# Node ranges of six edge tiles, groups of twelve, and one bank layout for both factors of K

## The chip, the cores and the metric

The kernel runs on one core of one Trainium2 chip. The metric is the device time of one execution in microseconds (us); several executions are timed, and the median counts.

## The reference

One layer of graph attention with 12500 nodes and 212500 edges, 128 features, 8 heads of 16 features, followed by a batch norm, a residual and a layer norm. The edges are sorted by their destination `dst`. Cut to what matters:

```python
Q, K, V = x @ WQ, x @ WK, x @ WV              # per node, split into 8 heads
Eh = edge_attr @ WE                           # per edge
score = K[src] * Q[dst] / 4 * Eh              # per edge and feature
score = exp(clip(score.sum(-1), -5, 5))       # per edge and head
wV = segment_sum(V[src] * score, dst)         # per node
Z = segment_sum(score, dst)
h = x + wV / (Z + 1e-6)
y = batch_norm(h) over the nodes              # mean and variance over all 12500 nodes
return layer_norm(x + y)
```

## The kernel before

**Tiles, ranges, groups.** The edges lie in T = 1661 tiles of 128, an edge on each partition. A range of nodes (`WN` = 64 nodes at most) takes `U` = 4 consecutive tiles, and a group is two ranges, `G` = 8 tiles; a range's nodes are found by one-hot matrices, so the ranges follow the sorted edges. There are 208 groups, the last of them with 5 tiles. A second path for edges that don't fit the ranges hangs on a flag and doesn't run here.

**Table stage.** TensorE multiplies the node columns `hx` by `w_kv` (line 900), ScalarE and VectorE copy the results out (`evac`, lines 454 and 455), and SyncE stores them to the table `kvd` in HBM, a row of K and V (1 KB) for each node, 512 nodes in each of 25 steps. Meanwhile POOL fetches rows of `x` for the first `NX` = 8 groups. These are turned by TensorE (`turn_x`, line 470) and projected (`project`, line 477) into K and V directly: three early groups in pieces of four tiles inside the table stage, at the steps that the list `piece` sets, the other five (called late here) inside the main loop, one group ahead of use. The list `steps` puts small setup jobs between the table's steps (`locate`, `place`, `locate_ring`, the first loads and `turned_onehot`).

**Fetches.** For each later group `load_kv` queues one indirect DMA for each tile (`gather`, line 290) on POOL: 128 rows of `kvd` by the indices `srcs`. The rows land in a slot of SBUF for eight tiles; there are `NSLOT` = 8 slots, and one more (`first`), which serves the table stage until group 6 is through. Four slots first hold `x` for two groups each. A slot goes back to the list `free` when `message(g)` has read it, or, for `x`, when the second of its two groups is projected (line 480). From group 12 on `pace` ties each queued fetch to a step of the iteration in which it is queued; what is queued is taken in order by POOL. In some groups the last tile isn't fetched: ScalarE copies node columns (`fetch_cols`, line 383, 32 a group) that TensorE then projects (`cols_mm`, line 420), VectorE does the same at 12 columns a group (`fetch_v`, line 364), and SyncE fetches rows one by one (`fetch_rows`, 8 a group).

**Main loop.** In iteration g VectorE makes `products(g)` (line 790: K times the edge factor out of two banks `ps_e`, then times the query factor out of two banks `ps_q`), `scores(g)` (797), the clip (806), `turned_onehot(g + 2)` (738), the share of group g - 2 (842 to 849), `onehot(g + 1)` (730 and 731), `message(g)` (812) and `fetch_v`. TensorE makes the factors of group g + 1 (`eh_mm`, 765, and `qe_mm`, 774), `cols_mm`, the sum `add_x(g - 3)` (858), the queries (748) and `gather_sum(g - 1)` (833). ScalarE makes the exponentials (807 into the bank `ps_m`, 808) and the copies of sums. The edge attributes `ea` come by SyncE, 1 MB for two groups (line 700); the places `rb` of the nodes, which `turned_onehot` compares, come from HBM too (line 600).

**PSUM.** Eight banks: three of `ps_e`, two of `ps_q`, `ps_m` (exponentials), `ps_i` (the index row `iota` for the one-hot) and `ps_a` (sums and queries).

**Order.** The order on each engine is that of the program; each engine takes its own instructions in that order, and semaphores join them.

**The end.** After the last group VectorE aggregates the statistics, and the last stage forms residual and layer norm for 25 blocks of 512 nodes. The summed nodes that had been stored to `hT` come back into free slots (`load_x`).

## Time and profile before

| | us |
|---|---|
| runs shown, median of 3 | 2052.56 (2050.99 to 2053.51) |
| the profiled execution | 2056.0 |
| its span | 2054.1 |
| TensorE matmul busy | 1612.4 (78%) |
| VectorE busy | 1645.6 (80%) |
| ScalarE busy | 1046.3 (51%) |
| POOL busy | 1535.1 (75%) |

PE is TensorE's matmul, PEld its weight load, DVE VectorE, ACT ScalarE, POOL GpSimd, SP SyncE. Busy is the sum of an engine's instructions; a bound can stand in a queue that is not busy all the time, since the step from one instruction to the next counts too. In a row of the timeline the bracket is the idle time ahead of it and what ended it; "issue" means that the profile shows nothing that the engine waited for. An fp32 matmul stands as two instructions.

### The profile page before, as it was taken

Reading aid. Unit: us, or ns where it says so; the run is one execution under the profiler, and the core shown is the slowest. Engines: PE = TensorE matmul, PEld = TensorE weight load, DVE = VectorE, ACT = ScalarE, POOL = GpSimd, SP = SyncE. Lnnn points to the kernel's source line nnn. Section 1 sums busy time; section 2 is a strip of 40 time slices with the busy share of each in tenths; the row PEclk is TensorE's granted clock in tenths of the full one; section 3 lists DMA queues with packets and bytes.
Section 4 is the critical chain, followed back from the end, with each engine's and each line's share of the span. In section 5 each row is a group of like instructions: output and inputs, shape, how many; then the busy total and the mean of one; then the engine's idle time right before and its main releaser. Section 6 shows DMA issues by size and latency. Waiting matters only on the chain.

```text
span 2054.1 us, 58951 instructions
## 1 busy us (share of the span) xinstructions
PE 1612.4 (78%) x12867; PEld 1300.0 (63%) x12867; DVE 1645.6 (80%) x5263; ACT 1046.3 (51%) x8290; POOL 1535.1 (75%) x1618
## 2 busy tenths in 40 slices
PE   7889888878777787777787877887877777777777
PEld 6777666666555665665566665666666666655666
DVE  4468999998887788788787887877877787877787
ACT  2245656664554555455455455454555555555436
POOL 7677777777777777777777777777777777777775
PEclk9899989998898888888888889888888898888899
DMA  7856655665555555555555556555555555555573
GB/s 262 294 174 186 205 184 174 200 203 168 172 184 176 173 184 168 175 183 168 181 182 178 170 170 190 179 162 186 184 159 187 183 158 185 165 178 184 170 245 128
DMA packets 130284, 377.69 MB, mean 184 GB/s; under 512 B 36112, under 2 KB 47547, under 8 KB 116091
## 3 DMA queue, kind: packets, MB, share of 16 engines
q0 software_dynamic: 74912, 203.26, 33.2%
q1 hardware_dynamic: 51816, 169.43, 24.2%
q14 instruction: 267, 2.18, 0.3%
q8 instruction: 103, 1.69, 0.3%
q10 hardware_dynamic: 3186, 1.13, 0.2%
HBM read 348.25 MB, written 25.44 MB: 182 GB/s over the span
## 4 chain that ended last, share of the span: by engine, by line
DVE 27%; DMA 25%; PE 20%; issue 19%; POOL 5%; ACT 2%; DVEq 2%; ACTq 0%; SPq 0%; POOLq 0%
DMA slot<-kvd,srcs 23%; DVE slot L790 9%; DVE s L797 8%; PE ps_q L774 5%; POOL slot L290 5%; PE ps_e L765 4%; PE ps_a L833 3%; DVE xv L364 2%; DVE ot L738 2%; PE ps_a L858 1%; DVEq L364 1%; DVE msg L812 1%; PE ps_e L900 1%; DVE s L806 1%; PE ps_q L900 1%
## 5 line engine op out<-in xcount | busy, mean ns | idle before, releaser
L290 POOL DMA_INDIRECT slot<-kvd,srcs x1518 | 1445.7, 952 | 467.0 <-issue 282.3
L383 ACT ACTIVATE xc<-hx 128x1 f32 x6272 | 647.0, 190 | 176.8 <-issue 142.6
L765 PE MATMUL ps_e<-w_e,ea 128*128 128x128 f32 x3322 | 496.7, 301 | 215.7 <-DVE slot L790 206.2
L765 PEld LDWEIGHTS ps_e<-w_e,ea 128*128 128x128 f32 x3322 | 431.6, 205 | 281.5 <-DVE slot L790 238.2
L774 PE MATMUL ps_q<-qs,ot 64*128 64x128 f32 x3322 | 374.3, 338 | 166.8 <-DVE slot L790 153.8
L790 DVE TENSOR_TENSOR slot<-slot,ps_e 128x512 f32<-128x512 f32 x410 | 273.2, 679 | 239.2 <-DMA slot<-kvd,srcs 202.0
L774 PEld LDWEIGHTS ps_q<-qs,ot 64*128 64x128 f32 x3322 | 303.5, 230 | 228.2 <-DVE slot L790 211.4
L833 PE MATMUL ps_a<-msg,oh 128*64 128x136 f32 x3322 | 316.5, 316 | 1.9 <-DVE msg L812 1.7
L807 ACT ACTIVATE ps_m<-s 128x64 f32<-128x64 f32 (+1 forms) x209 | 47.6, 228 | 500.6 <-DVE s L806 471.2
L797 DVE TENSOR_REDUCE s<-slot 128x64 f32<-128x1024 f32 (+1 forms) x208 | 249.9, 1202 | 19.4 <-DVE slot L790 0.9
L790 DVE TENSOR_TENSOR slot<-slot,ps_q 128x512 f32<-128x512 f32 x410 | 261.5, 678 | 1.0 <-PE ps_q L774 0.7
L833 PEld LDWEIGHTS ps_a<-msg,oh 128*64 128x64 f32 x3322 | 202.9, 150 | 88.4 <-issue 68.4
L812 DVE TENSOR_TENSOR msg<-slot,ps_m 128x1024 f32<-128x1024 f32 (+2 forms) x209 | 247.8, 1187 | 2.1 <-ACT ps_m L807 1.3
L876 ACT ACTIVATE ring<-ps_a 128x64 f32 x408 | 90.7, 222 | 155.1 <-PE ps_a L833 139.1
L364 DVE COPY xv<-hx 128x1 f32 x2304 | 155.8, 143 | 0.0
L731 DVE TENSOR_TENSOR oh<-ps_i,rel 128x512 f32<-128x512 f32 x208 | 141.7, 681 | 0.0
L858 PE MATMUL ps_a<-ident,at 128*128 128x128 f32 x408 | 112.5, 365 | 0.9 <-ACT os L838 0.9
L719 ACT ACTIVATE xw<-hx 128x64 f32 x416 | 82.4, 245 | 41.7 <-issue 23.6
L858 PEld LDWEIGHTS ps_a<-ident,at 128*128 128x128 f32 x408 | 81.6, 231 | 28.9 <-issue 5.6
L748 PE MATMUL ps_a<-w_q,xw 128*128 128x128 f32 x416 | 96.8, 321 | 0.4 <-ACT qs L752 0.4
L859 PE MATMUL ps_a<-xw,ident 128*128 128x128 f32 x408 | 95.8, 324 | 0.0
L738 DVE TENSOR_SCALAR ot<-rbq,wiota 128x512 f32<-128x512 uint8 x188 | 95.3, 507 | 0.0
(187 smaller groups left out, 1471.7 us busy)
## 6 DMA issues: line engine op xcount, KB each, us to landing
ea<-eaT SPq DMA_DIRECT2D x103, 1024.0 KB
byrow<-kvd SPq DMA_DIRECT2D x1536, 1.0 KB
slot<-kvd,srcs POOLq DMA_INDIRECT x1518
rbq<-relT SPq DMA_DIRECT2D x94, 128.0 KB
kvd<-slot SPq DMA_DIRECT2D x12, 512.0 KB
kvd<-t SPq DMA_DIRECT2D x12, 512.0 KB
ring<-xT SPq DMA_DIRECT2D x24, 256.0 KB
hT<-ring SPq DMA_DIRECT2D x23, 256.0 KB
```

What stands on the lines that cost most here:

```text
L290: return nc.gpsimd.indirect_dma_start(out=out, out_offset=None, in_=table, in_offset=bass.IndirectOffsetOnAxis(ap=part(SRC, e, 1), axis=0))
L364: nc.vector.tensor_copy(XV[k][:, r % P:r % P + 1], hx[:, ds(off, 1)])
L383: nc.scalar.activation(XC[k][:, r % P:r % P + 1], hx[:, ds(off, 1)], AF.Copy)
L731: by(("one", g), nc.vector.tensor_tensor(one, iota_ps[:, None, :WN].to_broadcast([P, k, WN]), r[:, :, None].to_broadcast([P, k, WN]), op=O ...
L738: by(("ot", g), nc.vector.tensor_scalar(OT[g], RB[g], wiota, None, op0=OP.is_equal))
L765: by(("eh", g), nc.tensor.matmul(t[:, j - a, :], EA[g][:, j, :], w_e, start=True, stop=True))
L774: by(("qe", g), nc.tensor.matmul(QE[g][h][:, j, :], OT[g][r, j * P:(j + 1) * P], QS[g][r], start=True, stop=True))
L790: step = nc.vector.tensor_tensor(kv, kv, of[g][i][:, :b - a, :], op=OP.mult)
L797: step = nc.vector.tensor_reduce(SS[g][:, a:b, :], KV[g](a, b, 0).rearrange("p t (h d) -> p t h d", d=DH), axis=AX.X, op=OP.add)
L812: step = nc.vector.tensor_tensor(MSG[g][:, a:b, :P].rearrange("p t (h d) -> p t h d", d=DH), KV[g](a, b, P).rearrange("p t (h d) -> p t h ...
L833: by(("sum", g), nc.tensor.matmul(AGG[g][h * WN:(h + 1) * WN], OH[g][h * n + j], MSG[g][:, h * n + j, :], start=(j == 0), stop=(j == k - 1)))
L858: nc.tensor.matmul(ps, AT[g], ident, start=True, stop=False)
```

## The change

`U` becomes 6 and `G` 12, so that a range of 64 nodes takes six tiles and there are 139 groups instead of 208. The constants that count groups are rescaled: `NX` 6, so 72 tiles come from `x` (64 before), `NSLOT` 5 slots of twelve tiles (12 KB in each partition, 8 KB before), `LATE` 6. The fetch rates per tile are kept: 48 columns a group for ScalarE in three loads of 16, 18 for VectorE, 12 rows for SyncE. `EARLY` stays at 3 groups, which are now nine pieces of four tiles. The edge attributes are loaded for each group, 768 KB.

The two factors of K share six banks of four tiles (`FULL_BANKS`): four of `ps_e`, two of `ps_q`; two of the banks hold two tiles of each factor. `products` runs over the banks, one instruction for each where the tiles lie in a slot (for a late group, whose K and V lie in pieces of four tiles, two for some banks). The bank `ps_i` is gone: `iota` lies in `ps_m`, and so do the results of `cols_mm`, which were in a bank `ps_e`.

Core of the diff:

```diff
-G = 8
-U = 4
+G = 12
+U = 6
+B = 4
 WN = 64
 CH = 512
-NSLOT = 8
-NX = 8
+NSLOT = 5
+NX = 6
 EARLY = 3
-RUN = 64
+RUN = 48
 ROWS = P
-LATE = 8
+LATE = 6
 RQ = 4
 SEC = RUN * U
 RING = 1024
 MARGIN = 64
 PAD = 2 * MARGIN + WN
-COLS = 32
+COLS = 48
 LOAD = 16
-FIRST_COL = 8
+FIRST_COL = 6
 COL_LAG = 3
-SP_ROWS = 8
-FIRST_ROW = 8
+SP_ROWS = 12
+FIRST_ROW = 6
 ROW_LAG = 2
...
+FULL_BANKS = [("ps_e", (0, 1, 2, 3), "eeee"), ("ps_e", (4, 5, 6, 7), "qqee"), ("ps_e", (8, 9, 10, 11), "eeqq"),
+              ("ps_e", (4, 5, 10, 11), "eeee"), ("ps_q", (0, 1, 2, 3), "qqqq"), ("ps_q", (6, 7, 8, 9), "qqqq")]
...
-    small_ps = psp.tile([P, 4, P], F32, name="ps_m", bufs=1)
+    small_ps = psp.tile([P, 4 * P], F32, name="ps_m", bufs=1)
     sum_ps = psp.tile([P, 4 * P], F32, name="ps_a", bufs=1)
-    iota_ps, spare_ps = psp.tile([P, 4, P], F32, name="ps_i", bufs=1)[:, 0, :], sum_ps[:, W + P:W + 2 * P]
+    iota_ps, spare_ps = small_ps[:, 2 * P:3 * P], sum_ps[:, W + P:W + 2 * P]
 
     def exp_ps(g):
-        c = (g % 2) * G * H
-        return small_ps[:, 3, c:c + G * H].rearrange("p (t h) -> p t h", h=H)
+        c = 4 * P - (g % 2 + 1) * G * H
+        return small_ps[:, c:c + G * H].rearrange("p (t h) -> p t h", h=H)
 
 
...
-    first = slot(NSLOT).rearrange("p (h c d) -> p h c d", h=2, d=2 * P)
+    first = slot(NSLOT).rearrange("p (h c d) -> p h c d", c=B, d=2 * P)
 
     def table_tile(q):
-        return first[:, q % 4] if q % 4 < 2 else tab.tile([P, 4, 2 * P], F32, name="t", bufs=2)
+        return first[:, q % 6] if q % 6 < 3 else tab.tile([P, B, 2 * P], F32, name="t", bufs=3)
...
-            PAIRS[g] = edge_bank(g).rearrange("p a b -> p (a b)")[:, :2 * P]
+            PAIRS[g] = small_ps[:, :2 * P]
...
-        return psp.tile([P, 4, P], F32, name="ps_e", bufs=3)
+        return psp.tile([P, 4, P], F32, name="ps_e", bufs=PSUM["ps_e"])
...
-        if a and (g % 2 or g == nxg - 1):
+        if a == G - B and (g % 2 or g == nxg - 1):
...
-        for t in range(ustarts[r[0]], end, P):
-            n = min(P, end - t)
+        for t in range(ustarts[r[0]], end, P // G * G):
...
-                turned_of = wp.tile([P, P], F32, name="relby", bufs=1)
+                turned_of = xt_tile()[:, 0, :]
...
+    def banks(g):
+        if nt(g) == G:
+            return FULL_BANKS
+        return [(name, range(a, b), kind * (b - a)) for name, kind in (("ps_e", "e"), ("ps_q", "q"))
+                for a, b in halves(g)]
+
     def load(i):
...
-        gs = range(2 * i, min(2 * i + 2, NG))
-        if not gs:
-            return
-        t, n = wp.tile([P, 2, G, P], F32, name="ea", bufs=2), sum(nt(g) for g in gs)
-        assert nt(2 * i) == G or len(gs) == 1
-        for k, g in enumerate(gs):
-            EA[g] = t[:, k]
-        nc.sync.dma_start(t.rearrange("p c a b -> p (c a b)")[:, :n * P],
-                          eaT[:, starts[2 * i] * P:(starts[2 * i] + n) * P])
+        EA[i] = wp.tile([P, G, P], F32, name="ea", bufs=2)
+        nc.sync.dma_start(EA[i].rearrange("p a b -> p (a b)")[:, :nt(i) * P],
+                          eaT[:, starts[i] * P:(starts[i] + nt(i)) * P])
...
-        half = [table_tile(2 * (g % 2) + a) for a in (0, 1)]
-        KV[g] = lambda a, b, c, n=P: half[a // 4][:, a % 4:a % 4 + b - a, c:c + n]
-        for a in (0, 4):
+        part = [table_tile(3 * (g % 2) + a) for a in range(G // B)]
+        KV[g] = lambda a, b, c, n=P: part[a // B][:, a % B:a % B + b - a, c:c + n]
+        for a in range(0, G, B):
...
+    BANK, FACTOR = {}, {}
...
-        EH[g] = []
-        for a, b in halves(g):
-            t = edge_bank(g)
-            for j in range(a, b):
-                by(("eh", g), nc.tensor.matmul(t[:, j - a, :], EA[g][:, j, :], w_e, start=True, stop=True))
-            EH[g].append(t)
+        BANK[g] = []
+        for name, tiles, kinds in banks(g):
+            BANK[g].append(psp.tile([P, B, P], F32, name=name, bufs=PSUM[name]))
+            for k, (j, kind) in enumerate(zip(tiles, kinds)):
+                FACTOR[kind, g, j] = BANK[g][-1][:, k, :]
+                if kind == "e":
+                    by(("eh", g), nc.tensor.matmul(FACTOR["e", g, j], EA[g][:, j, :], w_e, start=True, stop=True))
     def qe_mm(g):
-        QE[g] = [psp.tile([P, 4, P], F32, name="ps_q", bufs=2) for _ in (0, 1)]
         for j in range(U):
             for h in (0, 1):
                 if j < usizes[2 * g + h]:
                     r = slice(h * WN, (h + 1) * WN)
-                    by(("qe", g), nc.tensor.matmul(QE[g][h][:, j, :], OT[g][r, j * P:(j + 1) * P], QS[g][r],
-                                                   start=True, stop=True))
+                    by(("qe", g), nc.tensor.matmul(FACTOR["q", g, h * usizes[2 * g] + j],
+                                                   OT[g][r, j * P:(j + 1) * P], QS[g][r], start=True, stop=True))
...
-        return halves(g) if g < nxg and g not in SLOT else [(0, sizes[g])]
-
-    def products(g, hs=(0, 1)):
-        for of in (EH, QE):
-            for i in hs:
-                a, b = halves(g)[i]
-                kv = KV[g](a, b, 0)
-                step = nc.vector.tensor_tensor(kv, kv, of[g][i][:, :b - a, :], op=OP.mult)
-                PARTS.setdefault(g, []).append(step)
+        return [(a, a + B) for a in range(0, G, B)] if g < nxg and g not in SLOT else [(0, sizes[g])]
+
+    def in_runs(g, tiles):
+        runs = [[tiles[0], tiles[0] + 1]]
+        for j in tiles[1:]:
+            if j == runs[-1][1] and (g in SLOT or j % B):
+                runs[-1][1] += 1
+            else:
+                runs.append([j, j + 1])
+        return runs
+
+    def products(g, which=None):
+        for i, (_, tiles, _) in enumerate(banks(g)):
+            if which is not None and i not in which:
+                continue
+            by_k, runs = BANK[g][i][:, :len(tiles), :], in_runs(g, tiles)
+            if g in SLOT and len(runs) == 2:
+                (a, b), (c, d) = runs
+                n = b - a
+                assert c - a == G // 2 and d - c == n
+                kv = KV[g](0, G, 0).rearrange("p (h t) d -> p h t d", h=2)[:, :, a:b, :]
+                step = nc.vector.tensor_tensor(kv, kv, by_k.rearrange("p (h t) d -> p h t d", h=2), op=OP.mult)
+            else:
+                k = 0
+                for a, b in runs:
+                    kv = KV[g](a, b, 0)
+                    step = nc.vector.tensor_tensor(kv, kv, by_k[:, k:k + b - a, :], op=OP.mult)
+                    k += b - a
+            PARTS.setdefault(g, []).append(step)
...
-    for k in range(2 * early):
-        piece.setdefault(3 + k * (NQ - 4) // (2 * early), []).append((k // 2, 4 * (k % 2)))
+    for k in range(G // B * early):
+        piece.setdefault(3 + k * (NQ - 4) // (G // B * early), []).append((k // (G // B), B * (k % (G // B))))
...
-        if g % 2:
-            load((g - 1) // 2 + 2)
+        within(load, g + 2)
...
-            turn_x(g + 1, 0, True)
-            turn_x(g + 1, 4, True)
+            for a in range(0, G, B):
+                turn_x(g + 1, a, True)
...
-            for step in (SENT[g - 1], PARTS[g][1], BY["eh", g + 1], PARTS[g][3], PARTS[g][4], BY["qe", g + 1]):
+            for step in (SENT[g - 1], PARTS[g][0], PARTS[g][1], BY["eh", g + 1], *PARTS[g][2:7], BY["qe", g + 1]):
...
-        fetch_cols(g, 1)
+        for k in range(1, COLS // LOAD):
+            if k > 1:
+                load_cols(g, k)
+            fetch_cols(g, k)
...
-    products(g, (0,))
+    products(g, (0, 1, 2))
```

Three places in the order of the built programs, where the argument rests.

POOL at the end of the fetches from `x` (table `x`, indices `srcs`), with what each instruction waits for (DMAHW and DMASW are transfers, DVE is VectorE). Before:

```order
L290 DMA slot_124<-x,srcs 128x128 [waits DMASW5_49,DVE_49]
L290 DMA slot_124<-x,srcs 128x128 [waits DMASW6_49]
L290 DMA slot_124<-x,srcs 128x128 [waits DMASW7_49,DVE_49]
L290 DMA slot_631<-kvd,srcs 128x256 [waits DMAHW4_49,DMAHW3_49,DMAHW5_49,DMAHW2_49,DMAHW6_49,DMAHW1_49,DMAHW7_49,DMAHW0_49,DMASW0_49]
L290 DMA slot_631<-kvd,srcs 128x256 [waits DMASW1_49]
```

And after:

```order
L295 DMA slot_122<-x,srcs 128x128 [waits DMASW6_49]
L295 DMA slot_122<-x,srcs 128x128 [waits DMASW7_49]
L295 DMA slot_786<-kvd,srcs 128x256 [waits DMAHW3_49,DMAHW4_49,DMAHW2_49,DMAHW5_49,DMAHW1_49,DMAHW6_49,DMAHW0_49,DMAHW7_49,DMASW0_49,DVE_49]
L295 DMA slot_786<-kvd,srcs 128x256 [waits DMASW1_49]
L295 DMA slot_786<-kvd,srcs 128x256 [waits DMASW2_49]
```

The first fetch from `kvd` waited for transfers alone; it now carries a wait on VectorE too, the last reader of its slot. Two groups' fetches (16) stood ready before without such a wait on `message`; the slots of the first two groups are now freed by `message(0)` and `message(1)`.

VectorE behind the table's end, group 0 (`oh` is the one-hot, `ot` its counterpart by node, `s` the scores). Before:

```order
L730 TENSOR_TENSOR oh<-rel,lim 128x1
L731 TENSOR_TENSOR oh<-ps_i,rel 128x512
L790 TENSOR_TENSOR slot_195<-slot_195,ps_e 128x4x128 [waits PE_49] x2
L790 TENSOR_TENSOR slot_195<-slot_195,ps_q 128x4x128 [waits DVE_49,PE_49] x2
L797 TENSOR_REDUCE s<-slot_195 128x64 [waits DVE_49]
L806 TENSOR_SCALAR s<-s 128x64 [waits DVE_49]
L738 TENSOR_SCALAR ot<-rb,wiota 128x512 [waits DMAHW6_49,DMAHW5_49]
L730 TENSOR_TENSOR oh<-rel,lim 128x1
L731 TENSOR_TENSOR oh<-ps_i,rel 128x512
L812 TENSOR_TENSOR msg<-slot_195,ps_m 128x8x128 [waits Activation_49]
```

And after:

```order
L735 TENSOR_TENSOR oh<-rel,lim 128x1
L736 TENSOR_TENSOR oh<-ps_m,rel 128x768
L811 TENSOR_TENSOR slot_192<-slot_192,ps_e 128x4x128 [waits PE_49] x3
L806 TENSOR_TENSOR slot_192<-slot_192,ps_e 128x2x2x128 [waits DVE_49]
L811 TENSOR_TENSOR slot_192<-slot_192,ps_q 128x4x128 x2
L819 TENSOR_REDUCE s<-slot_192 128x96 [waits DVE_49]
L828 TENSOR_SCALAR s<-s 128x96 [waits DVE_49]
L743 TENSOR_SCALAR ot<-rb,wiota 128x768 [waits DMAHW7_49,DMAHW0_49]
L735 TENSOR_TENSOR oh<-rel,lim 128x1
L736 TENSOR_TENSOR oh<-ps_m,rel 128x768 [waits Activation_49]
L834 TENSOR_TENSOR msg<-slot_192,ps_m 128x12x128
```

The same steps in the same order, with six products instead of four, over 12 tiles instead of 8; the one-hot reads `iota` in `ps_m` and waits for ScalarE, whose exponentials go to that bank.

VectorE in an iteration with `cols_mm` (16 before, 12 after), from the clip on (`rz`, `at` are the share of group g - 2). Before:

```order
L806 TENSOR_SCALAR s<-s 128x64 [waits DVE_49]
L738 TENSOR_SCALAR ot<-rbq,wiota 128x512
L842 TENSOR_SCALAR rz<-os 128x8 [waits Activation_49]
L845 RECIPROCAL rz<-rz 128x8 [waits DVE_49]
L849 SCALAR_TENSOR_TENSOR at<-os,keep,rz 128x128 [waits DVE_49,PE_49]
L730 TENSOR_TENSOR oh<-rel,lim 128x1 [waits PE_49]
L731 TENSOR_TENSOR oh<-ps_i,rel 128x512
L812 TENSOR_TENSOR msg<-slot_1399,ps_m 128x8x128 [waits Activation_49]
```

And after:

```order
L828 TENSOR_SCALAR s<-s 128x96 [waits DVE_49]
L743 TENSOR_SCALAR ot<-rbq,wiota 128x768
L864 TENSOR_SCALAR rz<-os 128x8 [waits Activation_49]
L867 RECIPROCAL rz<-rz 128x8 [waits DVE_49]
L871 SCALAR_TENSOR_TENSOR at<-os,keep,rz 128x128 [waits DVE_49,PE_49]
L735 TENSOR_TENSOR oh<-rel,lim 128x1 [waits PE_49]
L736 TENSOR_TENSOR oh<-ps_m,rel 128x768 [waits PE_49]
L834 TENSOR_TENSOR msg<-slot_1715,ps_m 128x12x128
```

The one-hot had no wait of its own; it now waits for TensorE, which writes the result of `cols_mm` into the same bank.

## Rows read from the trace of the kernel before

**Rows 1.** Page: busy us (share) xcount; a group: busy us, mean ns | idle.

```profile
PE 1612.4 (78%) x12867; PEld 1300.0 (63%) x12867; DVE 1645.6 (80%) x5263; ACT 1046.3 (51%) x8290; POOL 1535.1 (75%) x1618
...
L290 POOL DMA_INDIRECT slot<-kvd,srcs x1518 | 1445.7, 952 | 467.0 <-issue 282.3
```

**Rows 2.** Timeline, POOL, head and end: start us, duration us, what, [idle before].

```profile
3.21 1.15 POOL L290 DMA_INDIRECT slot<-x,srcs  x1 [2.04 <-DMA srcs<-src]
...
85.32 0.94 POOL L290 DMA_INDIRECT slot<-x,srcs  x1 [0.30 <-issue]
...
90.95 0.94 POOL L290 DMA_INDIRECT slot<-kvd,srcs  x1 [4.69 <-issue]
92.20 0.95 POOL L290 DMA_INDIRECT slot<-kvd,srcs  x1 [0.30 <-issue]
...
1998.01 0.95 POOL L290 DMA_INDIRECT slot<-kvd,srcs  x1 [0.30 <-issue]
```

**Rows 3.** Waits: who waited for whom: us in total, times, longest us.

```profile
DVE slot L790 <- DMA slot<-kvd,srcs: 202.0, 116, 5.4
...
POOL slot L290 <- DVE slot L790: 47.8, 157, 0.3
```

**Rows 4.** Timeline, PE, table stage: transposes L470, projections L477, table L900.

```profile
13.28 0.60 PE L470 MATMUL ps_e<-ident,slot 128*128 128x128 f32 x4
...
15.69 1.03 PE L477 MATMUL ps_q<-w_kv,xt 128*128 128x256 f32 x4
...
17.41 1.09 PE L900 MATMUL ps_q<-w_kv,hx 128*128 128x256 f32 x4
...
66.53 2.07 PE L477 MATMUL ps_q<-w_kv,xt 128*128 128x256 f32 x4 [5.24 <-ACT xt L454]
```

**Rows 5.** Timeline, DVE, group 0, behind the table's end.

```profile
86.44 0.14 DVE L730 TENSOR_TENSOR oh<-rel,lim 128x1 f32<-128x1 f32 x1
86.50 0.68 DVE L731 TENSOR_TENSOR oh<-ps_i,rel 128x512 f32<-128x512 f32 x1
87.10 1.27 DVE L790 TENSOR_TENSOR slot<-slot,ps_e 128x512 f32<-128x512 f32 x2
89.82 1.22 DVE L797 TENSOR_REDUCE s<-slot 128x64 f32<-128x1024 f32 x1
91.07 0.19 DVE L806 TENSOR_SCALAR s<-s 128x64 f32<-128x64 f32 x1
...
95.89 0.51 DVE L738 TENSOR_SCALAR ot<-rb,wiota 128x512 f32<-128x512 uint8 x1 [4.63 <-DMA rb<-relT]
...
97.00 1.20 DVE L812 TENSOR_TENSOR msg<-slot,ps_m 128x1024 f32<-128x1024 f32 x1
```

**Rows 6.** Stretch 400:1800: busy us by engine, PEclk, DMA; two DVE groups.

```profile
400.00:1800.00 1400.00, 1084.24 (x8700) 864.26 (x8696) 1134.71 (x3767) 725.38 (x6039) 1060.47 (x1115) 0.86 0.57 177
...
L797 DVE TENSOR_REDUCE s<-slot 128x64 f32<-128x1024 f32 x149 | 181.7, 1220 | 14.5 <-DVE slot L790 0.9
...
L849 DVE SCALAR_TENSOR_TENSOR at<-os,keep,rz 128x128 f32<-128x128 f32 x148 | 51.9, 351 | 15.1
```

**Rows 7.** Timeline, PE: edges L765, places L774; last, the group of L420.

```profile
89.58 1.95 PE L765 MATMUL ps_e<-w_e,ea 128*128 128x128 f32 x16
...
91.46 1.16 PE L774 MATMUL ps_q<-qs,ot 64*128 64x128 f32 x16
...
1017.25 2.67 PE L774 MATMUL ps_q<-qs,ot 64*128 64x128 f32 x16 [3.00 <-DVE slot L790]
...
L420 PE MATMUL ps_e<-w_kv,xc 128*128 128x256 f32 x98 | 39.5, 489 | 0.0
```

**Rows 8.** Timeline, DVE, the last two groups.

```profile
1994.27 0.69 DVE L790 TENSOR_TENSOR slot<-slot,ps_e 128x512 f32<-128x512 f32 x1
...
2001.50 0.48 DVE L731 TENSOR_TENSOR oh<-ps_i,rel 128x320 f32<-128x320 f32 x1
...
2001.90 0.54 DVE L790 TENSOR_TENSOR slot<-slot,ps_e 128x384 f32<-128x384 f32 x1
```

More of the change, by code (lines that the diff above doesn't have):

```diff
@@ L316, in gnn_kernel @@
     tot = len(col_tiles) * P
-    assert -(-tot // (2 * COLS)) <= P and COLS == 2 * LOAD
+    assert -(-tot // (2 * COLS)) <= P and COLS % LOAD == 0
     col_ids = consts.tile([P, 2 * COLS], I32, name="col_ids")
@@ L560, in place @@
         end = ustarts[r[0]] + (r[1] - r[0]) * r[2]
-        for t in range(ustarts[r[0]], end, P):
-            n = min(P, end - t)
+        for t in range(ustarts[r[0]], end, P // G * G):
+            n = min(P // G * G, end - t)
             ps, of = spare_ps, rel(t, n)
@@ L672, in load_x @@
         k = 0
-        while k < 4 and todo and todo[0] in done:
+        while k < 2 * G * P // B4 and todo and todo[0] in done:
             XR[todo.pop(0)] = t[:, k * B4:(k + 1) * B4]
@@ L682, in new @@
         return XR[i] if i in XR else in_ring(i * B4, width(i))
-    EA, OH, OT, XW, BASE, MSG, QE, OS, AT, AGG = ({} for _ in range(10))
+    EA, OH, OT, XW, BASE, MSG, OS, AT, AGG = ({} for _ in range(9))
     def nt(g):
@@ L1089, in gnn_kernel @@
     sums_out(g - 1)
-    products(g, (1,))
+    products(g, (3, 4, 5))
     qe_mm(last)
@@ L1104, in gnn_kernel @@
     onehot(last)
-    products(last, (0,))
+    products(last, (0, 2))
     scores(last, 0)
     clip_exp(last, 0)
-    products(last, (1,))
+    products(last, (1, 3))
     add_x(g - 1)
```

10 lines of the change are left out of this document (4 added, 6 removed).

## The prediction

> **What bounds the kernel now.** I read the page's busy shares first: no engine is over 80%, and POOL's largest line is the row fetch [rows 1]. A share does not show a bound, so I went to POOL's own timeline. There each fetch (one indirect DMA for one tile of 128 edges) takes 0.94 to 0.95 us with 0.30 us before it, and the next one starts 1.25 us after the last [rows 2]. From the first fetch out of the table `kvd` at 90.95 us to the last at 1998.01 us there are 1518 of them, so 1517 steps in 1907.1 us, 1.257 us each: the queue is never empty. Where POOL's idle time is put down to another engine, the longest single wait is 0.3 us, that is the ordinary gap [rows 3]. On the other side VectorE waited 202.0 us in all for fetched rows [rows 3]. So the time is built of three stretches: the **head** until the first fetch from `kvd` (90.95 us), **1518 fetches at 1.257 us**, and the **tail** after the last one (2054.1 - 1998.01 = 56.1 us). Work on VectorE, ScalarE and TensorE counts only where it moves one of the three.
>
> **The number of fetches.** T is 1661 tiles. Before, 64 tiles come from `x` and are projected, 79 are put together without POOL (49 from columns by ScalarE, 12 rows by SyncE, 18 columns by VectorE), and 1661 - 64 - 79 = 1518 are left. After, the tables give 48, 12 and 17, so 77, and six groups of 12 make 72 from `x`: 1661 - 72 - 77 = 1512. Six fewer at 1.257 us: **-7.5 us**. The eight more fetches from `x` cost POOL 8 x 1.25 = 10 us in the head. Before, they ran from 3.21 to about 86.3 us [rows 2]; after they would end at 96 us or a little later, and the next paragraph says why POOL could not use those 10 us anyway.
>
> **When the first fetch from `kvd` may start.** Before, at the table's end the pool of eight slots held one that was never taken and one already emptied, so POOL waited only for the table's store, from 86.3 to 90.95 us [rows 2]. After, five slots hold three pairs of `x` and the first two early groups; the third early group takes the slot of the first pair. None is left. The first fetch then waits for VectorE, for `message(0)`, the last reader of group 0's slot. I price that chain from before's rows of the same place [rows 5]. From the start of group 0's flag (86.44 us): flag and one-hot 0.66 us, with 256 more columns 0.93 (a column costs 1.04 ns: this line took 0.68 us for 512 and, in the tail, 0.48 for 320 [rows 5, 8]); four products 2.72 us, six 4.08; the sum over features 1.25 us, with 512 more columns 1.78; the clip 0.25. That is 7.04 us to `turned_onehot(2)`. There before waited: its places landed at 95.89 us, 9.45 us after the flag, behind an edge transfer of 1 MB. That transfer is 0.75 MB now, so I take 8.4 us (bounds 7.04, no wait, and 9.45, as before). Then the places, flag and one-hot, 1.11 us before, 1.65 now; `message` 1.20, now 1.73; POOL's gap 0.30. Sum: 8.4 + 1.65 + 1.73 + 0.3 = 12.1 us behind the table's end, where before needed 4.5.
>
> **The table stage itself.** Three early groups are now nine pieces of four tiles instead of six. A piece is four transposes, 0.60 us, and a projection, from 15.69 to 17.41 us [rows 4], so 2.3 us of TensorE, which feeds the whole stage; three make 7.0. One of the three falls where TensorE stood 5.24 us for ScalarE [rows 4], and I count it as hidden. A third transpose in `place`, a shorter `locate` (278 ranges instead of 416) and the smaller edge transfer I put at zero together. So the table ends 4.6 us later (bounds 1.5, if two of the pieces hide, and 8). The first fetch from `kvd` starts at 86.44 + 4.6 + 12.1 = 103.1 us: **+12.1 us** (bounds 86.44 + 1.5 + 10.7 = 98.7, so +7.7, and 86.44 + 8 + 13.1 = 107.6, so +16.6). Later slots come in time: groups 1 and 2 free theirs every 10 us, and POOL needs 15 for 12 fetches.
>
> **The groups.** POOL takes 11 x 1.257 = 13.8 us for a group with one tile put together elsewhere, 15.1 us for the others. VectorE was busy 1134.71 us in 1400 us with 149 groups [rows 6], 7.6 us each; 1.5 times that is 11.4 us, and less for what is done once a group. It fits with 2.4 us to spare, so the saved work is worth **0**. All six banks now belong to one group, so the next one's matmuls can't start before this one's products. At the higher clock they need 24 x 0.122 + 24 x 0.073 = 4.7 us [rows 7], while VectorE has some 7 us of other work.
> One new wait: the projection of put-together tiles (`cols_mm`) now writes the bank in which the one-hot's `iota` lies, so in 65 groups VectorE's `onehot` waits until TensorE is through with it. After the last product that is at most 4.0 (1.5 times the 2.67 us that 16 instructions took at the lower clock) + 1.0 for `cols_mm` (2 x 0.489) = 5.0 us [rows 7]. VectorE gets there after the sum, 1.78, the clip, 0.25, the places, 1.5 x 0.51 = 0.75, and the share of an earlier group, of which one of three steps is 0.351 [rows 5, 6] and which I estimate at 0.8, so 3.6 in all: a wait of up to 1.4 us, with `message` and the next products queued behind it. Under POOL's 13.8 us a sum of 11.4 + 1.4 = 12.8 is hidden; uncovered, 65 x 1.4 = 91 us.
> [...]
>
> **The tail.** The last group has five tiles in both. The one ahead of it grows from 8 to 12. Before, its first product started at 1994.27 us and the last group's at 2001.90 [rows 8]. In these 7.6 us come two more products (1.36 us), and 512 more columns in the sum and in `message` (0.53 each): **+2.4 us** (bounds 0.5, since VectorE was partly early, and 4).
>
> **Sum.** 12.1 - 7.5 + 2.4 = +7.0 us. The span of 2054.1 becomes 2061.1. The profiled run took 2056.0 us, 3.4 over the median of the three runs, 2052.56; against the median the forecast is **2059.6 us**. Bounds: 7.7 - 7.5 + 0.5 = +0.7 and 16.6 - 7.5 + 4 = +13.1, so 2053.3 to 2065.7.
>
> **Rivals.** 0.2%, about what a measurement here can tell from no change, is 4.1 us: slower begins at 2056.7, faster below 2048.5.
> *The head hides it (not slower).* If the extra pieces fall into TensorE's waits and the places land before VectorE asks, the first fetch starts near 98.7 us and the six fetches pay for it: 2053.3. It decides at 100.2 us: a first fetch from `kvd` ahead of that and I am wrong. For it: the wait of 5.24 us is there. Against: the chain on VectorE alone is 10.7 us. Chance 0.22.
> *The fetches run closer.* 1.257 us is over the 1.25 of a plain step; that is 10 us in the run, from scattered steps. If other traffic made them and it goes, 2059.6 - 10 = 2049.4. Nothing I see removes it. Chance 0.08.
> *TensorE at its lower clock becomes the bound.* It stands still longer in each group, and the granted clock was already 0.86 on the mean [rows 6]. [...] It decides where TensorE leaves the higher level for a whole group, and before it did so only for parts of one. Chance 0.06.
> *Fewer, larger instructions make it faster.* 69 groups go, each with, for one, a step of 0.351 us [rows 6], 24 us, if VectorE set the pace: 2052.6 - 24 = 2028.6. VectorE's waits for rows [rows 3] speak against it. Chance 0.03. [...]
> The forecast keeps 0.61. Slower: 0.61 + 0.06, less 0.01 for its lower edge; same: 0.22 and most of 0.08; faster: the rest. The range, 2052 to 2067, spans the bounds and a little of the second rival, and leaves out about 0.15.
>
> **What would show it.** Right: POOL's fetches still 1.25 us apart with 1512 of them, the first from `kvd` at about 103 us after an idle stretch that VectorE's `message(0)` ends, the last at about 103 + 1511 x 1.257 = 2002.4 us, VectorE's waits for rows grown beyond 202 us, and a tail of 58.5 us. Wrong: gaps of microseconds between fetches later on (then slots or groups bound it), or a first fetch under 100.2 us.

## The result and the profile after

| | before | changed |
|---|---|---|
| timed executions, median | 2052.19 us (2050.99 to 2053.60, 6 runs) | 2061.25 us (2059.07 to 2064.99, 6 runs) |
| ratio to before | | 1.0047, 95% interval 1.0034 to 1.0060 |
| profiled execution, span | 2056.0, 2054.1 | 2059.07, 2057.3 |

The change costs about 0.5%. The median lies 1.7 us above the forecast, but the profile shows that it came about by another sum. The page of the changed kernel (busy us, share, count of instructions; then the largest group: busy us, mean ns | idle ahead of it):

```profile
PE 1449.7 (70%) x12201; PEld 1253.0 (61%) x12201; DVE 1560.4 (76%) x4529; ACT 942.2 (46%) x7577; POOL 1538.0 (75%) x1620
...
L295 POOL DMA_INDIRECT slot<-kvd,srcs x1512 | 1441.1, 953 | 464.7 <-issue 300.1
```

Against [rows 1], TensorE, VectorE and ScalarE all have less to do, and POOL has the same. POOL's timeline of the changed kernel (start, duration, what, idle before), as [rows 2]:

```profile
93.27 0.94 POOL L295 DMA_INDIRECT slot<-x,srcs  x1 [0.30 <-issue]
98.48 0.94 POOL L295 DMA_INDIRECT slot<-kvd,srcs  x1 [4.27 <-DVE msg L834]
99.73 0.95 POOL L295 DMA_INDIRECT slot<-kvd,srcs  x1 [0.30 <-issue]
...
1999.09 0.95 POOL L295 DMA_INDIRECT slot<-kvd,srcs  x1 [0.30 <-issue]
```

There are the 1512 fetches, the idle stretch that `message(0)` ends, and a step of (1999.09 - 98.48) / 1511 = 1.2578 us; no step is over 1.65 us, so POOL never stood empty again. The three stretches, for two profiles of each kernel (the second ones come from the runs below):

| us | before | before again | changed | changed again |
|---|---|---|---|---|
| first fetch from `kvd` | 90.95 | 91.05 | 98.48 | 97.85 |
| first to last fetch | 1907.06 | 1905.33 | 1900.61 | 1902.48 |
| one step | 1.2571 | 1.2560 | 1.2578 | 1.2591 |
| behind the last fetch | 56.1 | 54.9 | 58.2 | 56.5 |
| span | 2054.1 | 2051.3 | 2057.3 | 2056.8 |

On the mean the head grew by 7.2 us, six fetches fewer took off 7.5, longer steps gave back 2.9 (1511 x 0.0019), and the tail grew by 1.8: 4.4 in all. The timed medians lie 9 us apart. The other 5 us are a matter of which executions were profiled: before's two stood 3.8 and 0.2 us above the median of their series, the changed kernel's two 2.2 and 4.3 below theirs.

The waits of the changed kernel (who for whom: us in all, times, longest), as [rows 3]:

```profile
DVE slot L811 <- DMA slot<-kvd,srcs: 167.2, 96, 5.8
DVE s L828 <- issue: 151.5, 60, 2.8
...
PE ps_m L425 <- ACT ps_m L829: 62.6, 38, 3.3
...
DVE oh L736 <- PE ps_m L425: 7.0, 18, 1.3
```

VectorE still waits for fetched rows. The second row, 60 waits ahead of the clip, is new; it is taken up at the end. The last row is the new wait of the one-hot on the shared bank: 18 times, at most 1.3 us, under the 1.4 that the prediction allowed. The row shown ahead of it is the other side of that bank, `cols_mm` behind the exponentials. Both are hidden under POOL.

### The profile page after: what moved, and what is told of

It is laid out like the page before. It is cut to its first block, busy times and chain, and to the rows that moved or that the text cites. A ratio compares the mean times of both kernels' runs of the same rounds, so it can differ in the third digit from the quotient of the medians.

```text
span 2057.3 us, 55096 instructions
## 1 busy us (share of the span) xinstructions
PE 1449.7 (70%) x12201; PEld 1253.0 (61%) x12201; DVE 1560.4 (76%) x4529; ACT 942.2 (46%) x7577; POOL 1538.0 (75%) x1620
## 4 chain that ended last, share of the span: by engine, by line
DVE 28%; DMA 25%; issue 18%; POOL 11%; PE 10%; DVEq 5%; ACT 3%; ACTq 0%; POOLq 0%; SPq 0%
DMA slot<-kvd,srcs 23%; POOL slot L295 11%; DVE slot L811 10%; DVE s L819 7%; DVEq L360 4%; PE ps_e L769 3%; DVE slot L806 3%; DVE ot L743 2%; DVE xv L369 1%; PE ps_q L776 1%; PE ps_a L855 1%; DVE msg L834 1%; ACT xc L388 1%; DVE s L828 1%; PE ps_q L922 1%
## 5 line engine op out<-in xcount | busy, mean ns | idle before, releaser
L769 PE MATMUL ps_e<-w_e,ea 128*128 128x128 f32 x3322 | 610.9, 357 | 477.1 <-DVE slot L811 336.3
L769 PEld LDWEIGHTS ps_e<-w_e,ea 128*128 128x128 f32 x3322 | 562.6, 262 | 529.9 <-DVE slot L811 300.4
L811 DVE TENSOR_TENSOR slot<-slot,ps_e 128x512 f32<-128x512 f32 x412 | 265.8, 678 | 182.9 <-DMA slot<-kvd,srcs 167.2
L819 DVE TENSOR_REDUCE s<-slot 128x96 f32<-128x1536 f32 (+2 forms) x140 | 239.4, 1711 | 12.2 <-DVE slot L811 0.5
L834 DVE TENSOR_TENSOR msg<-slot,ps_m 128x1536 f32<-128x1536 f32 (+2 forms) x141 | 238.1, 1691 | 1.6 <-ACT ps_m L829 1.3
L776 PE MATMUL ps_q<-qs,ot 64*128 64x128 f32 x2218 | 186.3, 310 | 0.0
L811 DVE TENSOR_TENSOR slot<-slot,ps_q 128x512 f32<-128x512 f32 x275 | 174.8, 676 | 0.1
L776 PEld LDWEIGHTS ps_q<-qs,ot 64*128 64x128 f32 x2218 | 158.5, 212 | 21.2 <-issue 8.0
L828 DVE TENSOR_SCALAR s<-s 128x96 f32<-128x96 f32 (+1 forms) x140 | 31.3, 223 | 154.8 <-issue 151.5
L736 DVE TENSOR_TENSOR oh<-ps_m,rel 128x768 f32<-128x768 f32 (+1 forms) x139 | 131.6, 947 | 7.3 <-PE ps_m L425 7.0
L806 DVE TENSOR_TENSOR slot<-slot,ps_e 128x512 f32<-128x512 f32 x135 | 92.7, 687 | 4.6
L776 PE MATMUL ps_e<-qs,ot 64*128 64x128 f32 x1104 | 92.5, 281 | 0.0
```

What stands on the lines that cost most here:

```text
L736: by(("one", g), nc.vector.tensor_tensor(one, iota_ps[:, None, :WN].to_broadcast([P, k, WN]), r[:, :, None].to_broadcast([P, k, WN]), op=O ...
L769: by(("eh", g), nc.tensor.matmul(FACTOR["e", g, j], EA[g][:, j, :], w_e, start=True, stop=True))
L776: by(("qe", g), nc.tensor.matmul(FACTOR["q", g, h * usizes[2 * g] + j], OT[g][r, j * P:(j + 1) * P], QS[g][r], start=True, stop=True))
L806: step = nc.vector.tensor_tensor(kv, kv, by_k.rearrange("p (h t) d -> p h t d", h=2), op=OP.mult)
L811: step = nc.vector.tensor_tensor(kv, kv, by_k[:, k:k + b - a, :], op=OP.mult)
L819: step = nc.vector.tensor_reduce(SS[g][:, a:b, :], KV[g](a, b, 0).rearrange("p t (h d) -> p t h d", d=DH), axis=AX.X, op=OP.add)
```

## The experiments

**Both kernels again, unaltered.**

> The changed kernel once more, unaltered. Its profiled run took 2059.07 us, 3.2 more than the sum of before's own profiled span allows for (head +7.5, fetches -6.5, tail +2.1), while the medians of the timed runs lie 9.1 apart and its other five runs reach 2065. Theory A (POOL's queue of fetches bounds every execution): median 2060 to 2063; in this profile the first fetch from kvd again starts at 98 to 99 us, the tail is 58 us, and any further time lies in the 1511 steps between fetches, as many steps of 1.6 us or a pause, not in the head or the tail. Rival B (the head varies, because group 0's chain waits for transfers): the first fetch then starts anywhere from 98 to 104 us and the span follows it one for one. Rival C (the tail varies): the last fetch at 1999 us and a tail of up to 64.

> The kernel before, unaltered, for a second profile. Its first profile had a span of 2054.1 us with the run at 2056.0, above all six timed runs (2051.0 to 2053.6). If that one was a long execution, this one has a span near 2050, and theory A says that the 4 us lie in the steps between fetches (1.2571 us on the mean then, 1.2545 now), rival B that they lie ahead of the first fetch (90.95 us then, 87 now), rival C that they lie in the tail (56.1 us then, 52 now).

The changed kernel took 2062.90 us (2058.56 to 2065.12) where before took 2053.01, ratio 1.0052 (1.0039 to 1.0065); before's second profiled execution took 2053.16. The spans are in the table above. Theory A wants what differs between two executions in the steps alone, and the profiles do not show that: before's second one is 2.8 us shorter, 1.7 of it in the steps and 1.2 in the tail, and the changed kernel's second one has 1.9 us more in its steps but 0.6 less in the head and 1.7 less in the tail. The head or tail that varies by 6 us of rivals B and C is not seen either. The profiled execution of the changed kernel was the shortest of its series both times, so what makes a typical one longer stands in no profile.

**Undo the wait at the table's end.**

```diff
-EARLY = 3
+EARLY = 2
```

> Two early groups in place of three, so that one of the five slots is untaken at the table's end and the first fetch from kvd needs no message(0). If the wait for VectorE is what moved the head, the first fetch starts at about 94.5 us (the fetches from x end at 94.2, the table is stored at 90), 4 us ahead of the changed kernel, and since there are as many fetches the time falls by 4 us: 2057. If the head does not set the end, because VectorE catches up or falls behind later by itself, the time stays at 2061. If two early groups leave VectorE later instead (one group less done ahead of the table's end), it could lose the 4 us again in waits later in the run, and the steps between fetches would show pauses.

Measured: 2062.18 us (2060.44 to 2064.66), ratio 1.0047: no gain. POOL's timeline of this run:

```profile
93.98 1.11 POOL L295 DMA_INDIRECT slot<-x,srcs  x1 [0.30 <-issue]
95.39 0.95 POOL L295 DMA_INDIRECT slot<-kvd,srcs  x1 [0.30 <-issue]
...
158.74 0.94 POOL L295 DMA_INDIRECT slot<-kvd,srcs  x1 [3.21 <-PE ps_e L475]
...
190.08 0.94 POOL L295 DMA_INDIRECT slot<-kvd,srcs  x1 [2.83 <-DVE msg L834]
```

The first wait is gone, and the first fetch starts 3.1 us ahead of the changed kernel's. Two later waits for a slot, 2.9 and 2.5 us over the usual 0.3, take more than that back. The timeline of VectorE in the same run shows why slots come late:

```profile
150.90 0.69 DVE L811 TENSOR_TENSOR slot<-slot,ps_e 128x512 f32<-128x512 f32 x1 [5.26 <-ACT xw L724]
154.22 1.95 DVE L811 TENSOR_TENSOR slot<-slot,ps_e 128x512 f32<-128x512 f32 x4 [2.63 <-PE ps_e L776]
```

A group that is projected inside the loop passes TensorE, ScalarE, TensorE and VectorE in turn, and VectorE stands 5.3 + 2.6 us for it: 16.2 us from one such group's first product to the next (150.90 to 167.08), where POOL needs 15.1 for twelve fetches. So the head is not set by the wait at its start alone. With five slots of twelve tiles two things are nearly even there, and to remove one exposes the other.

**Fewer fetches.**

```diff
-COLS = 48
+COLS = 64
```

> 64 columns in place of 48 are put together in each iteration, so that ScalarE makes 64 tiles in place of 48 and POOL fetches 1496 in place of 1512. Theory A (POOL's queue bounds): 16 fetches fewer at 1.257 us, so -20 us: 2041. Theory B (VectorE or another engine paces the groups): nothing is saved, 2061, or more, since ScalarE and TensorE get more work (2048 copies of one column, 16 projections). ScalarE is busy 46% and its 2048 copies of 0.14 us or so add 290 us, or 14%; if that makes ScalarE's copies of put-together tiles late, POOL shows pauses and the gain is less than 20.

Measured: 2043.56 us (2038.24 to 2045.57), ratio 0.9948 (0.9934 to 0.9963): 19.3 under the changed kernel timed beside it, 1.21 us for each fetch saved, and faster than both kernels. POOL's first and last fetch from `kvd`:

```profile
100.15 0.94 POOL L295 DMA_INDIRECT slot<-kvd,srcs  x1 [4.07 <-DVE msg L834]
...
1983.86 0.95 POOL L295 DMA_INDIRECT slot<-kvd,srcs  x1 [0.30 <-PE ps_a L855]
```

The 2048 column copies more on ScalarE and the 16 projections on TensorE cost nothing that shows. Theory A holds: POOL's queue is the bound, and what the groups save elsewhere is worth nothing.

**What lengthens a step.** Of the 1512 fetches in the changed kernel's profile 63 are longer than 1.00 us, by 10.8 us in all over 0.95, the longest 1.34. The engines around one of them (timeline of the changed kernel):

```profile
1143.08 0.94 POOL L295 DMA_INDIRECT slot<-kvd,srcs  x1 [0.30 <-PE ps_a L880]
...
1144.24 0.61 DVE L743 TENSOR_SCALAR ot<-rbq,wiota 128x768 f32<-128x768 uint8 x1
1144.33 1.34 POOL L295 DMA_INDIRECT slot<-kvd,srcs  x1 [0.30 <-DVE s L828]
...
1145.97 0.95 POOL L295 DMA_INDIRECT slot<-kvd,srcs  x1 [0.31 <-DVE oh L735]
```

`ot`, the turned one-hot, began 0.09 us ahead of the fetch and ended at 1144.85; the fetch ended at 1145.67, 0.82 us later. Of the 63, 60 run beside an `ot`, and each of these ends 0.11 to 0.13 us or 0.81 to 0.83 us after it; of the 64 in before's first profile it is 56. What sets these two distances no run shows. I counted over all rows which of VectorE's operations ran beside a fetch: `ot` beside 168 fetches, 68 of them lengthened (over 0.975 us), by 10.7 us over 0.95; the products that read PSUM (`slot<-slot,ps_e`, line 811) beside 401, two lengthened. The three of the 63 that have no `ot` beside them, these two among them, end 0.81 to 0.82 us behind another operation of VectorE from SBUF to SBUF (lines 563, 645, 653). In the kernel before it is the same with the smaller `ot`: 226 beside, 59 lengthened, by 8.6 us. One of them:

```profile
1153.61 0.48 DVE L738 TENSOR_SCALAR ot<-rbq,wiota 128x512 f32<-128x512 uint8 x1
...
1153.71 1.20 POOL L290 DMA_INDIRECT slot<-kvd,srcs  x1 [0.30 <-issue]
```

Two things set `ot` apart from the products and the one-hot: it takes all its data from SBUF, where they have an operand in PSUM, and it takes 0.49 ns a column ((633 - 507) ns / 256, from the mean of its 124 and 188 instructions) against 1.04 for the one-hot. That one of the two makes the long fetches was my guess from the rows; why 100 of the 168 fetches beside an `ot` are not lengthened no run shows. To test it, `ot` gets an operand out of PSUM, a column of `iota` that holds 1.0; the result is unchanged.

```diff
-            by(("ot", g), nc.vector.tensor_scalar(OT[g], RB[g], wiota, None, op0=OP.is_equal))
+            one = iota_ps[:, 1:2].to_broadcast([P, U * P])
+            by(("ot", g), nc.vector.scalar_tensor_tensor(OT[g], RB[g], wiota, one, op0=OP.is_equal, op1=OP.mult))
```

> The kernel of ot_psum a third time, for its price on a chip on which the kernel before takes about 2053 us. Theory: the fetches that ran beside the one-hot are 0.95 us long like the others, the excess over 1511 x 1.25 us falls from 11 to 13 us to 1 to 3, and the time from 2062 to about 2052; the spread of the executions shrinks from 6.5 us to 3 or less. Rival: VectorE's longer group (1.2 us more) makes POOL wait for slots in pauses of microseconds, 2062 or more. If the kernel before takes over 2600 us again, the run repeats ot_psum and ot_psum2 and the price stays open.

Measured: 2053.71 us (2052.82 to 2058.03, 12 runs) where before took 2056.67 (2051.76 to 2058.15, 17 runs), ratio 0.9995 (0.9986 to 1.0003). The changed kernel was not timed beside it; in its own two series it stood at 1.0047 and 1.0052, so by the ratios the edit takes 0.5%, some 11 us, off it. Its groups (POOL's fetches and `ot`) and its waits:

```profile
L295 POOL DMA_INDIRECT slot<-kvd,srcs x1512 | 1434.4, 949 | 465.1 <-issue 303.8 <-DVE slot L812 40.5 <-DMA slot<-kvd,srcs 36.3
...
L744 DVE SCALAR_TENSOR_TENSOR ot<-rbq,wiota,ps_m 128x768 f32<-128x768 uint8 x124 | 125.7, 1014 | 39.9 <-ACT ps_m L830 38.6 <-DMA ea<-eaT 1.3
```

```profile
DVE slot L812 <- DMA slot<-kvd,srcs: 77.6, 48, 5.7
```

and one fetch beside the new `ot`, in its timeline:

```profile
1153.57 1.01 DVE L744 SCALAR_TENSOR_TENSOR ot<-rbq,wiota,ps_m 128x768 f32<-128x768 uint8 x1 [0.32 <-ACT ps_m L830]
...
1153.99 0.95 POOL L295 DMA_INDIRECT slot<-kvd,srcs  x1 [0.30 <-DMA slot<-kvd,srcs]
```

Now 214 fetches run beside `ot` and none is over 1.00 us; 8 of all are, 63 before the edit. The 8 are no stray ones: each ends 0.82 to 0.83 us behind an operation of lines 564 or 653, which read two operands from SBUF. One of them, with its fetch:

```profile
585.59 0.46 DVE L564 TENSOR_TENSOR rel<-rel,base_f 128x288 f32<-128x288 f32 x1
...
585.74 1.14 POOL L295 DMA_INDIRECT slot<-kvd,srcs  x1 [0.30 <-DVE rel L563]
```

With 0.46 us for 288 columns it is slower by the column than the old `ot` (0.61 us for 768). The edit made `ot` slower and gave it an operand out of PSUM at once, but by these rows it is not slowness that makes an operation harmless.

The first fetch comes at 99.34, the last at 1993.56: 1894.2 us, 1.2536 a step. The span is 2051.3. `ot` takes 0.38 us more and waits 0.32 for the exponentials in that bank; in all VectorE spends some 90 us more on it, and its waits for rows fall by the same 90 us (167.2 to 77.6), which is what slack looks like. One thing came out otherwise: the executions still spread over 5 us. And the span is only 5.5 to 6 us under the changed kernel's two, where the ratio gives 11. Most of that difference is a longer plain step: the mean of the steps under 1.3 us is 1.2527 us in this profile and 1.2504 in the four of the table, 3.5 us over 1511 steps, and before, timed beside it, took some 4 us more than in the other two series. Without it the edit is worth 9 to 9.5 us in the profiles, near the 10.7 and 12.4 us by which `ot` lengthens fetches in the changed kernel's two profiles, so the timed gain asks for no more long fetches than those profiles hold. What sets the plain step is not known: two runs on the chip of the next section have 1.2524 and 1.2525, four others there 1.2497 to 1.2500.

**The runs on other chips.** Seven runs fell on two chips (six on one, `cols64_ot_psum` on the other) where the kernel before takes 2614 to 2656 us. The waits of the kernel before there:

```profile
ACT xc L383 <- issue: 653.6, 1013, 1.5
...
PE ps_a L833 <- issue: 288.1, 302, 2.8
```

and TensorE in one group's sum, whose instructions on the usual chip follow without a gap:

```profile
1010.20 0.28 PE L830 MATMUL ps_a<-msg,oh 128*1 128x136 f32 x1 [1.15 <-issue]
1011.63 0.60 PE L833 MATMUL ps_a<-msg,oh 128*64 128x136 f32 x4 [1.15 <-issue]
```

TensorE stands between two instructions with nothing in the trace to wait for. ScalarE's idle time ahead of its column copies was 142.6 us in the first profile on the usual chip, and in part its own sequencer shows what fills it: there 104 us lie beside loads of column numbers and 8 beside register operations, here 104 and 289, since register operations, each 0.04 us or less there, take up to 1.40 here (515 of 6272 over 0.6 us). TensorE's granted clock over 400 to 1800 us is lower as well, 0.77 where it was 0.86; what makes these chips slow was not tested. POOL's queue runs empty (264 of its 1517 steps in this profile take 2 to 4 us), so it is not the bound there, and no price of a fetch can be read from these runs.

> The kernel before, unaltered, profiled as the first program on a chip: the profiles of the changed kernel (spans 2057.3 and 2056.8) were the first and shortest of their series, those of before (2054.1 and 2051.3) were not, which may be why the profiles lie 4.4 us apart on the mean and the medians 9. If so, this span is 2047 to 2049, with fewer or shorter long steps between fetches (excess over 1.25 us of 5 to 7 us in all, where the other two had 10.2 and 8.4), the first fetch from kvd again at 91.0 and a tail of 54 to 56. If the span is 2051 to 2054 again, the profiles' 4.4 and the medians' 9 differ by chance of the draw.

> The changed kernel, unaltered, profiled behind other programs of the same call, for the question under before_first. If later executions are longer, the span is 2060 to 2063 where the two first ones had 2057.3 and 2056.8, and the 4 to 6 us more lie in long steps between fetches (excess 15 to 18 us where those had 11.2 and 13.0), with the first fetch from kvd at 98 us and a tail of 57 to 58. If they lie in the tail, the last fetch is at 2000 and the tail 60 to 63.

2645.52 and 2738.58 us, one execution each: the changed kernel is 3.5% slower there. Why it loses more than before was not tested, and the question of the profiles (first or late in a series) was not answered by them.

> The turned one-hot of VectorE (ot) reads a second operand, a 1.0 out of PSUM, by which it multiplies; the result is the same. Theory: of the 1512 fetches some 60 take 1.05 to 1.34 us in place of 0.95, and nearly all of them run beside ot, each ending 0.82 us or 0.11 us after ot's end; the products, which read PSUM, are beside 388 fetches and lengthen none. If ot, an SBUF-to-SBUF operation at 0.4 ns a column, keeps POOL out while it runs, then with a PSUM operand the long fetches are gone and the excess of 11 to 13 us over 1511 x 1.25 falls to 2 or 3: about -9 us, 2052. ot itself takes 0.9 us in place of 0.61, which VectorE has to spare. Rival 1 (the long fetches come from DMA traffic or from the small rz operations that run beside them too): no change, 2061. Rival 2 (any ot that reads SBUF keeps POOL out for as long as it runs): the fetches beside it grow to 1.6 us, and the time rises by some 8 us.

> The kernel of ot_psum again (the turned one-hot reads a 1.0 out of PSUM), on a chip on which the kernel before takes about 2052 us; in the runs ahead of this one it took 2650 on theirs, where POOL's queue stands empty between groups and fetches are not the bound, so they could show only that of the fetches beside ot none is long any more (42 of 115 before), not what that is worth. Theory: the long fetches go, the steps' excess over 1.25 us falls from 11 to 13 us to 2 or 3, and the time from about 2062 to 2052; the spread between executions (2058.6 to 2065.1 for the changed kernel), which by this theory is how often a fetch and ot happen to meet, becomes smaller too. Rival: the fetches are shorter, but VectorE, with 1.2 us more for ot and its wait for the exponentials in each group, becomes late and POOL waits for it: 2062 or more.

2749.01 (2743.28 to 2751.55) and 2723.24 us (2718.99 to 2726.38, before 2618.51). The long fetches beside `ot` are gone here as well (over 0.975 us: none of the 168 beside it in the first run, one of 173, by 0.03 us, in the second; 50 of 155 in the changed kernel on this chip), and the time doesn't fall, as it should not where POOL isn't the bound.

> The same edit in the kernel before, where iota has a bank of its own. Its 1518 fetches have an excess of 8.4 to 10.2 us, of which some 8 are those beside ot: by the theory 2052.5 - 7 = 2045. It also tells what makes the medians of the two kernels lie 9 us apart while their profiles lie 4.4 apart: if in typical executions the larger ot of the changed kernel (0.61 us in place of 0.51) meets more or longer fetches, then without that meeting the two kernels lie only 2 us apart (first fetch +7.2, six fetches fewer -7.5, tail +2), that is 2045 and 2047, or 2050 and 2052. Rival: they lie 9 apart again, and the difference has nothing to do with long fetches.

2622.42 us (2614.23 to 2625.10), ratio 1.0014 (1.0004 to 1.0023). On this chip it can't price the edit, so what `ot` costs the kernel before stays an estimate: the 7.2 to 8.6 us by which its profiles show fetches lengthened beside it.

**The sum over features twice**, in groups 10 to 128, on the same chip:

```diff
-        for a, b in ranges(g, h):
+        for a, b in ranges(g, h) * (2 if 10 <= g < NG - 10 else 1):
```

> VectorE's sum over features is done twice in groups 10 to 128, with the same result: 119 times 1.71 us, 203 us more of VectorE's time. Theory A (POOL paces the groups at 13.8 or 15.1 us, VectorE needs about 10.6 and waits for the rest): 12.3 us still fits, so 0 to +10, near 2061, and VectorE's waits for fetched rows fall from 167 us towards 0. Rival (VectorE with its waits for the matmuls of the single set of six banks is already the pace): +203, 2264. Between the two, the excess over 0 tells how much of the 3 us a group was really free.

2739.84 us (2729.57 to 2746.91) against 2738.58 for the changed kernel's one execution: 203 us of VectorE's time cost nothing clear of the spread. VectorE is not the bound there either, but the run can't say that POOL paces the groups, since there it does not; on the usual chip the 90 us of `ot_psum3` are the evidence that VectorE has slack.

**Both edits together.**

> The two edits together: 64 columns in place of 48 in each iteration (1496 fetches in place of 1512) and the turned one-hot with a 1.0 out of PSUM. On a chip on which the kernel before takes about 2053 us, cols64 alone took 2043.6 (19.3 below the changed kernel, by 16 fetches at 1.26 us). Theory: POOL's queue is the bound, and the fetches that run beside the one-hot make up most of the excess of 14.4 us over 1495 x 1.25 in its profile; without them the excess is 2 to 4 us and the time 2043.6 - 10 = 2033, which beats both kernels. Rival 1: VectorE, with 1.2 us more in each group (one-hot 1.0 us in place of 0.61, and 0.4 of waiting for the exponentials), becomes late, and POOL waits for slots: 2044 or more, with pauses of microseconds between fetches. [...]

2857.96 us (2848.34 to 2861.02), ratio 1.0775 (1.0754 to 1.0797), on the second of the slow chips. ScalarE's idle time ahead of its column copies ("issue") is 857.6 us, 720.9 in `ot_psum`, and the time is 109 us over that run's; that the 2048 copies more make it so long is likely, not tested. On the usual chip the two together were not run, and whether 19 and 11 us add up is open.

## Why the prediction was right, and where it was not

**The bound and the count.** Right. 1512 fetches, one step after another; 16 fetches fewer took 19.3 us off.

**The first fetch.** The mechanism was right: no slot is left, and `message(0)` ends the wait. The size was not: +7.5 us, not +12.1. The failed step is *the table ends 4.6 us later*. TensorE over the first 86 us (columns: window, then busy us of PE, PEld, DVE, ACT, POOL, PEclk, DMA share, GB/s), before and changed:

```profile
0.00:86.00 86.00, 68.89 (x278) 62.87 (x279) 31.91 (x70) 22.31 (x44) 60.94 (x70) 0.94 0.83 284
```

```profile
0.00:86.00 86.00, 72.83 (x319) 67.38 (x320) 35.22 (x80) 24.98 (x48) 62.28 (x72) 0.96 0.82 285
```

It did 3.9 us more in the same time, so what the pieces added went into its waits, where I had let only one of the three hide; the stall of [rows 4] is now 1.89 us. The shorter `locate` and the smaller edge transfer, which the sum put at zero, may have helped; no run separates them:

```profile
66.54 1.13 PE L482 MATMUL ps_q<-w_kv,xt 128*128 128x256 f32 x4 [1.89 <-ACT xt L459]
```

VectorE's chain behind the table, as [rows 5]:

```profile
85.83 0.15 DVE L735 TENSOR_TENSOR oh<-rel,lim 128x1 f32<-128x1 f32 x1
...
89.36 1.28 DVE L811 TENSOR_TENSOR slot<-slot,ps_e 128x512 f32<-128x512 f32 x2 [1.93 <-PE ps_e L776]
...
92.60 1.75 DVE L819 TENSOR_REDUCE s<-slot 128x96 f32<-128x1536 f32 x1
...
95.00 0.62 DVE L743 TENSOR_SCALAR ot<-rb,wiota 128x768 f32<-128x768 uint8 x1 [0.40 <-DMA rb<-relT]
95.53 0.15 DVE L735 TENSOR_TENSOR oh<-rel,lim 128x1 f32<-128x1 f32 x1
...
96.47 1.75 DVE L834 TENSOR_TENSOR msg<-slot,ps_m 128x1536 f32<-128x1536 f32 x1
```

The flag starts at 85.83, 0.6 us ahead of before's 86.44, and from there to the fetch it is 12.65 us where I had 12.1. `turned_onehot(2)` comes after 9.17, not 8.4: it waits little for its places, since VectorE now waits 1.93 us for the query factor.

**The step.** With a first fetch under 100.2 us the text calls itself wrong and gives 2053.3; the head did what that rival says, and the time was still 2061. Two things made up the gap, and one of them was luck. The sum kept the step of before, 1.257 us; it grew, by 2.9 us over the run in the profiles. The rival *the fetches run closer* had noted 10 us of scattered long steps, with nothing seen to cause them. The long fetches among them come with operations of VectorE from SBUF to SBUF, `ot` above all (60 of the 63 over 1.00 us ran beside it, and none in `ot_psum3`), which the change makes 1.25 times as long (507 to 633 ns): the longest fetch takes 1.34 us where it took 1.20.

The luck is in the way from the span to the median. The span was forecast at 2061.1 us and came at 2057.3 and 2056.8, some 4 us less, mostly the head's error less what the steps took back. For the median the sum then took off 3.4 us, because before's profiled execution stood that far above its median; the changed kernel's stood 2.2 and 4.3 us below theirs. So the median came out 1.7 us from the forecast by errors of opposite sign. No run shows why those executions lie where they do, and what a typical execution of the changed kernel has beyond its profiles stays open.

**The groups.** Right in the verdict: saved work was worth nothing, and the bank wait was hidden. But VectorE's waits for rows fell from 202.0 to 167.2 us, where growth beyond 202 was named as a sign. In its place VectorE stands 151.5 us ahead of the clip, 60 times. The waits call it "issue", but VectorE's own sequencer shows what it is: the load of the column numbers for `fetch_v` into registers, which stands between the sum and the clip (count, shortest/median/longest in ns), after and before:

```profile
L360 DVEq TENSOR_LOAD <-v_ids x121: 1564/1815/4303, 175.6 to 1843.9; - x121
```

```profile
L355 DVEq TENSOR_LOAD <-v_ids x192: 845/868/1117, 169.0 to 1932.4; - x192
```

It starts beside the sum, which takes 1.75 us. With 12 numbers it is through in that time. With 18, every second load (60 of the 121) takes 4.05 to 4.30 us, the others 1.56 to 1.82, and the clip waits for the long ones. Why every second one is long no run shows. POOL has no pause for it, so it costs nothing that shows.

**The tail.** Right: +2.4 forecast, +2.1 in the first pair of profiles and +1.6 in the second. The last group's first product starts later than in [rows 8], 5.8 us behind the last fetch (3.9 before):

```profile
1995.68 1.88 DVE L811 TENSOR_TENSOR slot<-slot,ps_e 128x512 f32<-128x512 f32 x3
...
2004.92 0.54 DVE L811 TENSOR_TENSOR slot<-slot,ps_e 128x384 f32<-128x384 f32 x1
```

**The other rivals.** TensorE's mean granted clock over 400 to 1800 us fell from 0.86 [rows 6] to 0.83, which bound nothing: POOL has no pause there. What a group costs with the clock at 0.50 throughout no run shows; the longest such stretch of the changed kernel is some 13 us (1950 to 1963 us), where POOL needs 13.8 or 15.1 for a group. Fewer and larger instructions brought down VectorE's busy time in that window from 1134.71 to 1086.46 us, and the time did not follow. The window's row of the changed kernel, with the columns of [rows 6]:

```profile
400.00:1800.00 1400.00, 960.71 (x8285) 825.48 (x8283) 1086.46 (x3356) 667.36 (x5679) 1060.56 (x1115) 0.83 0.58 177
```

## What to carry to other kernels

Where a queue of GpSimd's indirect DMAs is the bound, count its entries first, then look at its long steps and at what VectorE does beside them: here fetches of 0.95 us grew beside operations that take all their data from SBUF, to as much as 1.34 beside `ot` (0.49 ns a column) and 1.20 beside slower ones with two inputs; with an operand out of PSUM `ot` lengthened none beyond 1.00 us, and the 0.38 us that it took longer cost nothing that shows. A wait at a start is worth what the next limit behind it leaves, so ask what feeds the queue a hundred microseconds later. When work is added to a stage, look at all of the bounding engine's waits in it before charging that work to its end. Compare profiled executions with profiled ones and medians with medians: one profile can lie some us to either side of its series (here from 4.3 below the median to 3.8 above it), as much as this change is worth. And a wait put down to "issue" is not always without a cause: look at the loads of the engine's own sequencer, which took up to 4.30 us here.
